# A planned one-core graph kernel: the power iteration recorded ahead of the eigenvector solver, and a narrower window of groups while layer 0 ends

## The chip, the cores and the metric

The kernel runs on one core of a Trainium2 chip. A core has five engines with instruction streams of their own: TensorE (PE in the profile, with PEld for its weight loads), VectorE (DVE), ScalarE (ACT), GpSimd (POOL) and SyncE (SP), which here only issues DMAs. The metric is device time in microseconds, the median of several executions; one more execution is profiled, and every row quoted below comes from that one.

## The reference

The input x holds 128 graphs of 64 nodes with 256 features, in float32; all graphs share one 64x64 adjacency matrix. Four residual layers follow one another, each of them `x = x + f(relu(layernorm(x)))`:

- layer 0: two graph convolutions (`relu(adj @ (h W + b))`), and then, for p = 1, 2, 3, 4, an LSTM over windows of p successive nodes, whose last hidden state replaces the window's last node. The LSTM with p = 4 has four dependent steps;
- layer 1: a spectral graph convolution and an attention block. It needs the largest eigenvalue of the symmetrised adjacency: `L_norm = 2 L / lam_max - I`;
- layer 2: graph attention with an additive score;
- layer 3: a transform into the eigenvector basis of a normalised Laplacian (`U.T @ x`), two dense layers, and the transform back. It needs all 64 eigenvectors.

In short, what bears on this case:

```
x = x + layer0(h, adj, ...)                      # LSTMs, no eigenvalues
lam_max = eigvalsh(L)[-1] + 1e-8                 # layer 1
_, U = eigh(d^-1/2 (diag(deg) - A) d^-1/2)       # layer 3
```

## The kernel before

Nothing is issued as it is written. The code runs once against proxies that record every operation of every engine with its operands (`Plan.record`, line 114), and `Plan.issue` (line 338) then issues all of them in an order that `Plan.schedule` (line 227) works out with a list scheduler. All instructions therefore carry line 344 in the profile, and are told apart by their tiles.

Each recorded operation has a group. Layer 0 is done for eight groups of 1,024 rows (8 tiles of 128 rows), numbered 0 to 7 (`NG = 8`). Group 8 (`WEIGHTS`, line 1390) loads the weights of layers 1 to 3 over those of the LSTMs, and group 9 (`ATTN`) clears four attention tiles. Layers 1 to 3 are done for sixteen groups of 512 rows (4 tiles), numbered 10 to 25 (`REST = 10`, line 1612). The result of layer 0 goes through DRAM: a group of layer 0 writes `put[g]`, and two later groups read it back. The work on the adjacency matrix, the eigenvectors (`eig_decomp`, line 347) and the largest eigenvalue (a power iteration of 21 squarings, lines 1135 to 1156), is one long chain of small operations, mostly on VectorE, and forms group 1000 (`EIG`).

What sets the order:

- the scheduler repeatedly picks, over all engines, the operation that can start first. Among operations that could start at once it takes the lowest rank (`Plan.rank`, line 328): lower groups first, while group `EIG` comes first on TensorE and last on all other engines, and within `EIG` the operation that was recorded earlier comes first;
- an operation is considered only if its group is inside the window above the oldest unfinished group (line 256): `op.group >= oldest + window(oldest) + (op.eng == "SP")` is passed over. DMAs on SP may be one group ahead, and `EIG` is exempt;
- buffers come from pools: 12 tiles `big` of 512 KB, 10 `mid`, 14 `stat` and 8 PSUM banks. While a layer-0 group is the oldest, `reserve` (line 971) holds up to 7 `big` tiles back for it. Ten more `big` tiles are cut from `arena` once `EIG` is finished, and some from `Whh3`, `sums` and `mids` once layer 0 is.

The window before the change reads

```
return max(oldest, 0) + 2 - oldest if oldest < NG - 1 else max(oldest, REST) + 8 - oldest
```

so two groups of layer 0 overlap, and from the moment when group 7 is the oldest, groups up to 17 are inside: eight groups of layers 1 to 3.

Within layer 0, `lstm_step` (line 1213) and `lstm_fast` (line 1261) alternate matmuls into PSUM banks, gate functions on ScalarE and products on VectorE. A group of layers 1 to 3 begins with `fetch` (a DMA), `ln_stats` (line 1195: four `bn_stats` and four `bn_aggr` on VectorE, then four small operations on GpSimd), four ReLUs on ScalarE (`relu_norm`, line 1471) and `mix_fm`, a burst of 32 small matmuls against `lapb`, the scaled Laplacian that the largest eigenvalue gives. The projections with `Wc`, the attention and the rest follow in `layer1` (line 1485). Layer 3 uses `Ub` and `UTb`, the eigenvectors; group 8 also needs them (`ursum`, `C3`, lines 1417 to 1423).

Of the kernel before, what the change touches and what calls it, by code (L numbers as in the profile page):

```python
# [12 lines left out]
N = 64  # L13
# [874 lines left out]
P = 128  # L888
# [3 lines left out]
NG = NT // GT  # L892
HT = 4

SETUP, WEIGHTS, ATTN, REST, EIG = -1, NG, NG + 1, NG + 2, 1000
# [37 lines left out]
def gnn_kernel(ctx: ExitStack, tc: tile.TileContext, a, out):  # L933
# [4 lines left out]
    def C(shape, name):  # L938
        return pool.tile(list(shape), F32, name=name)
# [26 lines left out]
    more(mids, tuple(range(NG)))  # L966

    def window(oldest):
        return max(oldest, 0) + 2 - oldest if oldest < NG - 1 else max(oldest, REST) + 8 - oldest

    def reserve(kind, oldest):
        if oldest < NG:
# [3 lines left out]
    def slack(op):  # L976
        if op.eng == "PE":
            return 0.4 if op.group >= REST and op.group != EIG else 0.12
        return 0.05

    plan = Plan(tc, {"PE": nc.tensor, "V": nc.vector, "ACT": nc.scalar, "G": nc.gpsimd, "SP": nc.sync}, pools, late, reserve, window, EIG, REST + NT // HT - 6, slack)
    PE, V, ACT, G, SP = (plan.proxy(e) for e in ("PE", "V", "ACT", "G", "SP"))

    def bank(name):
        return plan.value("bank")
# [23 lines left out]
    adj2 = C([P, N], "adj2")  # L1009
    adjT2 = C([P, N], "adjT2")  # L1010
# [24 lines left out]
    ident = C([P, P], "ident")  # L1035
    G.iota(ident, pattern=[[1, P]], base=0, channel_multiplier=-1, allow_small_or_imprecise_dtypes=True)
    V.tensor_scalar(ident, ident, 0.0, None, op0=ALU.is_equal)
    ones = C([P, P], "ones")
# [8 lines left out]
    def blockdiag(t):  # L1047
        V.memset(t, 0.0)
        return t[:N, :N], t[N:, N:]
# [54 lines left out]
    Ublk, UTblk = blockdiag(Ub), blockdiag(UTb)  # L1104
    room = Carver(arena)

    QT, Vc, inner = eig_decomp(plan, room, adj2[:N], adjT2[:N], ident[:N, :N], ident, ones)
    for dst, lhs, rhs in ((Ublk, QT, Vc), (UTblk, Vc, QT)):
        l2 = inner.tile([P, 2, N])
        V.tensor_copy(l2, lhs.unsqueeze(1).to_broadcast([P, 2, N]))  # L1110
        pp = bank("U")
        PE.matmul(pp[:, :N], l2.rearrange("p r n -> p (r n)"), rhs, start=True, stop=True)
        V.tensor_copy(dst[0], pp[:N, :N])
        V.tensor_copy(dst[1], pp[N:, :N])


    def colsum(col):

        pt = bank("colsum")
        PE.matmul(pt[:, :1], ones, col, start=True, stop=True)  # L1120
        r = room.tile([P, 1])
        V.tensor_copy(r, pt[:, :1])
        return r
# [30 lines left out]
    V.reciprocal(lmax, lmax)  # L1154
    V.tensor_scalar(lmax, lmax, 2.0, None, op0=ALU.mult)
    V.scalar_tensor_tensor(lapb, adjTb, lmax, ident, op0=ALU.mult, op1=ALU.subtract)


    flat = lambda t: t.rearrange("p t f -> p (t f)")
# [231 lines left out]
    room = Carver(wih[1], whh[1], wih[2], whh[2], wih[0])  # L1391
# [282 lines left out]
```

## Time and profile before

| | |
|---|---|
| median of 3 runs | 2164.6 us (2164.06 to 2165.33) |
| the profiled execution | 2165.9 us, span 2164.1 us |
| TensorE busy | 2112.6 us, 98% of the span |
| VectorE / ScalarE / GpSimd busy | 1800.3 / 1079.8 / 653.1 us |
| matmuls | 16,580 |
| granted TensorE clock, mean | 0.996 |

The span runs from the first to the last instruction on the core. The busy times of an engine are the union of its instructions; two matmuls in the pipeline count once. The table of slices shows one long stretch of layer 0 up to about 1367 us and of layers 1 to 3 after that, with TensorE at nine tenths or more in all slices but the first and the last. A built program's order of instructions can be matched one for one with the trace, engine by engine, and so tells which group an instruction of line 344 belongs to.

### The profile page before, as it was taken

How to read it: one execution, taken by the hardware profiler on the slowest of the kernel's cores; microseconds unless marked ns; L12 is line 12 of the kernel's file. 1: busy time of each engine (PE TensorE's matmuls, PEld its weight loads, DVE VectorE, ACT ScalarE, POOL GpSimd, SP SyncE). 2: the span in 40 equal slices, each digit the busy share in tenths (PEclk: the TensorE clock that was granted, in tenths of full speed). 3: DMA queues.
4: the chain of work that ended last, by engine and by line, in shares of the span. 5: the costliest groups of instructions: out<-in, count | busy, mean ns of one | idle time of the engine just before them, and what ended most of it. 6: DMA issues, size and time to landing. Idle time of an engine off the chain costs nothing.

```text
span 2164.1 us, 45598 instructions
## 1 busy us (share of the span) xinstructions
PE 2112.6 (98%) x16580; PEld 1630.7 (75%) x16580; DVE 1800.3 (83%) x7402; ACT 1079.8 (50%) x2331; POOL 653.1 (30%) x968
## 2 busy tenths in 40 slices
PE   8999999999999999999999999999999999999997
PEld 6688688688678678678778688766777767776776
DVE  5888788889899999899989887568878868885797
ACT  3354354354354354345345345456566655645673
POOL 7221211210200110110110113654456745554353
PEclk9999999999999999999999999999999999999999
DMA  5000100100100100100000213000010000000001
GB/s 205 2 3 22 41 3 22 40 1 21 40 1 20 40 1 20 40 1 21 26 1 23 69 40 97 21 1 2 21 41 21 21 22 21 12 11 11 1 2 60
DMA packets 44866, 57.67 MB, mean 27 GB/s; under 512 B 8928, under 2 KB 38496, under 8 KB 44640
## 3 DMA queue, kind: packets, MB, share of 16 engines
q1 hardware_dynamic: 43536, 53.71, 7.6%
q8 instruction: 130, 2.13, 0.4%
q10 hardware_dynamic: 1104, 1.05, 0.2%
q14 instruction: 96, 0.79, 0.1%
HBM read 37.53 MB, written 16.78 MB: 25 GB/s over the span
## 4 chain that ended last, share of the span: by engine, by line
PE 83%; DVE 11%; POOL 2%; ACT 1%; DMA 1%; issue 1%; SPq 0%; DVEq 0%; ACTq 0%
PE bank L344 83%; DVE arena L344 3%; DVE big L344 3%; DVE stat L344 2%; DVE mids L344 1%; DVE sums L344 1%; POOL stat L344 1%; POOL sums L344 1%; DMA Wih<-in_WihT_dram 1%; ACT mids L344 0%; ACT arena L344 0%; DMA Whh<-in_L_b_dram 0%; DMA big<-put 0%; ACT big L344 0%; SPq L344 0%
## 5 line engine op out<-in xcount | busy, mean ns | idle before, releaser
L344 PE MATMUL bank<-big,Wih 128*128 128x256 f32 (+3 forms) x2400 | 748.2, 435 | 18.7 <-DVE arena L344 9.3
L344 PEld LDWEIGHTS bank<-big,Wih 128*128 128x128 f32 x2400 | 439.9, 190 | 205.0 <-issue 114.4
L344 ACT ACTIVATE mids<-bank,bl 128x256 f32<-128x256 f32 (+3 forms) x528 | 275.4, 528 | 407.3 <-PE bank L344 403.5
L344 PE MATMUL bank<-big,Whh 128*128 128x256 f32 (+2 forms) x1624 | 431.0, 368 | 3.5 <-DVE big L344 3.5
L344 DVE TENSOR_TENSOR arena<-arena 64x21 f32<-64x21 f32 (+5 forms) x2255 | 372.9, 196 | 35.8 <-POOL arena L344 8.2
L344 PEld LDWEIGHTS bank<-big,Whh 128*128 128x128 f32 x1624 | 294.3, 190 | 42.5 <-issue 10.1
L344 PE MATMUL bank<-big,sums 128*128 128x168 f32 (+2 forms) x1728 | 268.8, 307 | 0.0
L344 PEld LDWEIGHTS bank<-big,sums 128*128 128x128 f32 (+1 forms) x1728 | 225.4, 178 | 16.0 <-issue 3.9
L344 POOL TENSOR_SCALAR stat<-stat 128x4 f32<-128x4 f32 (+1 forms) x228 | 67.9, 299 | 485.4 <-DVE stat L344 472.5
L344 ACT COPY mids<-bank 128x168 f32<-128x168 f32 (+2 forms) x393 | 132.1, 357 | 138.1 <-PE bank L344 135.1
L344 DVE TENSOR_TENSOR big<-mids 128x512 f32<-128x512 f32 (+2 forms) x256 | 142.8, 565 | 31.3 <-ACT mids L344 28.6
L344 ACT ACTIVATE mids<-mids,bl 128x336 f32<-128x336 f32 (+2 forms) x192 | 102.4, 540 | 71.4 <-DVE mids L344 67.6
L344 DVE TENSOR_TENSOR mids<-bank,mids 128x168 f32<-128x168 f32 (+2 forms) x307 | 112.9, 372 | 25.8 <-PE bank L344 22.3
L344 DVE SCALAR_TENSOR_TENSOR arena<-arena 64x1 f32<-64x1 f32 (+15 forms) x565 | 120.9, 237 | 7.5 <-POOL arena L344 3.9
L344 POOL TENSOR_TENSOR big<-big 128x168 f32<-128x168 f32 (+1 forms) x24 | 16.8, 712 | 359.9 <-DVE arena L344 132.2
L344 POOL TENSOR_TENSOR stat<-stat,mhalf 128x4 f32<-128x4 f32 (+1 forms) x114 | 122.1, 1072 | 5.7
L344 ACT ACTIVATE mids<-big 128x256 f32<-128x256 f32 (+2 forms) x176 | 89.4, 509 | 67.7 <-DVE big L344 48.8
L344 PE MATMUL bank<-Wih,big 128*128 128x256 f32 (+1 forms) x512 | 111.7, 358 | 0.2 <-ACT big L344 0.2
L344 DVE TENSOR_SCALAR arena<-arena 64x1 f32<-64x1 f32 (+9 forms) x537 | 104.8, 202 | 8.4 <-POOL arena L344 0.8
L344 DVE TENSOR_TENSOR big<-big,mids 128x256 f32<-128x256 f32 (+2 forms) x200 | 99.3, 498 | 11.1 <-ACT mids L344 10.2
L344 PEld LDWEIGHTS bank<-Wih,big 128*128 128x128 f32 x512 | 87.7, 190 | 15.4 <-issue 4.5
L344 ACT COPY big<-bank 128x512 f32<-128x512 f32 x108 | 59.9, 587 | 55.9 <-PE bank L344 50.8
(357 smaller groups left out, 3568.0 us busy)
## 6 DMA issues: line engine op xcount, KB each, us to landing
big<-in_x_dram SPq DMA_DIRECT2D x30, 512.0 KB, 5.2
put<-big SPq DMA_DIRECT2D x16, 512.0 KB, 3.0
Wih<-in_WihT_dram SPq DMA_DIRECT2D x3, 1024.0 KB, 11.8
Whh<-in_WhhT_dram SPq DMA_DIRECT2D x3, 1024.0 KB, 13.8
big<-put SPq DMA_DIRECT2D x6, 512.0 KB, 5.8
arena<-put SPq DMA_DIRECT2D x6, 512.0 KB, 6.6
out_dram<-big SPq DMA_DIRECT2D x12, 256.0 KB, 2.3
out_dram<-arena SPq DMA_DIRECT2D x12, 256.0 KB, 2.3
```

Source lines behind the costliest of these rows:

```text
L344: getattr(self.engines[op.eng], name)(*map(real, args), **{k: real(a) for k, a in kw.items()})
```

## The change

Two edits. The call of `eig_decomp` and the lines that make `Ub` and `UTb` from its result move behind the power iteration, so that the power iteration's operations are recorded first and take their space in `arena` first. No operation is added or removed. And the window has three cases now: with one of groups 7, 8 and 9 the oldest, only group 10 is inside (group 11 for its DMA); from group 10 on, eight groups are, as before.

```diff
     def window(oldest):
-        return max(oldest, 0) + 2 - oldest if oldest < NG - 1 else max(oldest, REST) + 8 - oldest
+        return max(oldest, 0) + 2 - oldest if oldest < NG - 1 else REST + 1 - oldest if oldest < REST else 8
...
     room = Carver(arena)
-
-    QT, Vc, inner = eig_decomp(plan, room, adj2[:N], adjT2[:N], ident[:N, :N], ident, ones)
-    for dst, lhs, rhs in ((Ublk, QT, Vc), (UTblk, Vc, QT)):
-        l2 = inner.tile([P, 2, N])
-        V.tensor_copy(l2, lhs.unsqueeze(1).to_broadcast([P, 2, N]))
-        pp = bank("U")
-        PE.matmul(pp[:, :N], l2.rearrange("p r n -> p (r n)"), rhs, start=True, stop=True)
-        V.tensor_copy(dst[0], pp[:N, :N])
-        V.tensor_copy(dst[1], pp[N:, :N])
-
 
     def colsum(col):
...
     V.scalar_tensor_tensor(lapb, adjTb, lmax, ident, op0=ALU.mult, op1=ALU.subtract)
+
+
+    QT, Vc, inner = eig_decomp(plan, room, adj2[:N], adjT2[:N], ident[:N, :N], ident, ones)
+    for dst, lhs, rhs in ((Ublk, QT, Vc), (UTblk, Vc, QT)):
+        l2 = inner.tile([P, 2, N])
+        V.tensor_copy(l2, lhs.unsqueeze(1).to_broadcast([P, 2, N]))
+        pp = bank("U")
+        PE.matmul(pp[:, :N], l2.rearrange("p r n -> p (r n)"), rhs, start=True, stop=True)
+        V.tensor_copy(dst[0], pp[:N, :N])
+        V.tensor_copy(dst[1], pp[N:, :N])
```

## The prediction

> **What bounds the kernel now.** I read the page first, then busy time by stretch, then TensorE's waits where layer 0 ends, then the timelines of TensorE and VectorE at those waits.
>
> The page, engines:
>
> ```profile
> PE 2112.6 (98%) x16580; PEld 1630.7 (75%) x16580; DVE 1800.3 (83%) x7402; ACT 1079.8 (50%) x2331; POOL 653.1 (30%) x968
> ```
>
> TensorE is the bound, with 51.5 us of idle time in all; an edit that leaves its matmuls alone can win no more than part of that. Where it lies (stretch, length, then busy time and count of PE, PEld, DVE, ACT, POOL, the granted clock and the DMAs):
>
> ```profile
> 50.00:1200.00 1150.00, 1138.77 (x6765) 895.97 (x6764) 1023.94 (x5008) 520.75 (x1309) 161.80 (x289) 1.00 0.06 18
> 1200.00:1250.00 50.00, 46.36 (x182) 34.01 (x182) 43.26 (x200) 17.30 (x36) 10.79 (x20) 0.97 0.22 74
> 1250.00:1300.00 50.00, 45.96 (x259) 40.09 (x258) 44.99 (x187) 23.73 (x60) 5.72 (x9) 1.00 0.15 44
> 1300.00:1350.00 50.00, 49.00 (x257) 43.40 (x256) 37.82 (x180) 26.06 (x61) 15.03 (x16) 1.00 0.32 104
> 1350.00:1400.00 50.00, 46.63 (x633) 39.88 (x632) 27.12 (x72) 25.41 (x52) 32.00 (x44) 1.00 0.06 23
> 1400.00:1950.00 550.00, 541.19 (x5910) 395.82 (x5912) 440.76 (x1173) 326.00 (x567) 302.02 (x398) 1.00 0.06 17
> ```
>
> Between 1200 and 1400 us TensorE is idle for 12.0 us; this is where group 7 runs alone and layer 0 ends. The waits there, and TensorE's timeline around them:
>
> ```profile
> PE bank L344 <- DVE big L344: 5.3, 5, 2.5
> PE bank L344 <- issue: 3.4, 2, 1.7
> PE bank L344 <- DVE mids L344: 1.7, 2, 1.2
> PE bank L344 <- DVE arena L344: 1.6, 2, 1.2
> ...
> 1223.19 10.97 PE L344 MATMUL bank<-big,Wih 128*128 128x512 f32 x26 [1.16 <-DVE arena L344]
> 1237.51 0.78 PE L344 MATMUL bank<-big,Whh 128*128 128x256 f32 x2 [2.48 <-DVE big L344]
> 1264.10 7.33 PE L344 MATMUL bank<-big,Wih 128*128 128x336 f32 x26 [1.60 <-DVE big L344]
> 1363.00 1.16 PE L344 MATMUL bank<-lapb,big 64*64 64x64 f32 x64
> 1371.06 1.44 PE L344 MATMUL bank<-lapb,arena 64*64 64x64 f32 x83 [1.72 <-issue]
> ```
>
> Eight groups of layers 1 to 3 are allowed in from 1222 us, but their first matmul is the burst at 1363.00. In the trace, group 10 has its row statistics at 1230, while its ReLUs run at 1309.55: the eight inputs and the tiles reserved for group 7 leave no `big` tile for its result. So the wide window brings TensorE nothing before 1363. It brings VectorE work, though:
>
> ```profile
> 1228.41 0.43 DVE L344 BATCH_NORM_STATS2 stat<-big 128x6 f32<-128x256 f32 x1 [1.30 <-DMA big<-put]
> 1233.12 1.37 DVE L344 BATCH_NORM_STATS2 stat<-big 128x6 f32<-128x256 f32 x4
> 1236.80 0.66 DVE L344 TENSOR_TENSOR big<-mids 128x512 f32<-128x512 f32 x1
> ```
>
> The statistics of groups 10 to 13 stand between group 7's products (the row at 1236.80 is one), and the matmul at 1237.51 waits for that product. The chain's two values, last:
>
> ```profile
> L344 DVE SCALAR_TENSOR_TENSOR lapb<-adjTb,arena,ident x1: 333/333/333, 131.1 to 131.1; 128x128 f32<-128x128 f32 x1
> L344 DVE COPY Ub<-bank x2: 208/218/228, 1337.0 to 1337.2; 64x64 f32<-64x64 f32 x2
> ```
>
> `lapb` is there at 131 us, 1230 us before its first use; the eigenvectors at 1337, some 29 us before group 7 ends at 1366.6.
>
> [...]for 1.30 us VectorE sits before a `bn_stats` whose DMA is under way, with group 7's products behind it. [...]Here 2.48 us sufficed: the next ten 256-column matmuls start 0.43 us apart and not 0.216, so the gap costs 1.9 us more. [...]
>
> **The power iteration ahead.** No instruction is added or removed, and `lapb` isn't waited for: worth nothing by itself. But the eigenvector chain falls behind. By the order of instructions, ahead of group 6's last VectorE instruction stand 3,897 of group `EIG` before and 3,832 after. 65 x 0.19 us (small `arena` operations, start to start) = 12.4 us of VectorE work moves under group 7. The cover is the 29 us above; in the new order the chain's last matmul still has 11 us of matmuls after it before group 7 ends.
>
> **The narrow window, while layer 0 ends.** Three things move ahead of group 7's end, all of group 10: its burst (1.44 us by its usual pace), sixteen matmuls of 256 columns for `Wc` (x 0.216 = 3.46) and eight transposes (x 0.11 = 0.88), together 5.8 us of TensorE work. They stand about where TensorE waited 2.48, 1.60 and 0.69 us. The statistics of groups 11 to 13 (3 x 1.6 us of VectorE, start to start) leave the 1230s. Four group-7 matmuls of 0.86 us (3.4 us) slip from before group 6's last transpose to after it, which alone shifts work and wins nothing.
>
> The interval from group 6's last transpose (1220.2) to group 7's (1365.2) took 145.0 us for 131.2 us of matmuls at their usual spacing, so 13.8 us were idle or at the slow clock. After: 131.2 + 3.4 + 5.8, less the burst of group 10 that already stood there (1.4), = 139.0. Its first part, up to the first matmul of the eigensolver's last phase (before at 1292.65), decides. It held 60.8 us of matmuls in 72.5; VectorE had 65.9 us of work after group 6's four additions, and 4.8 us besides. After, it holds 74.0 us of matmuls and, counting instructions in the new order at their measured spacing, 74.5 us of VectorE. Adding the additions (1.8) and, say, 4 us of VectorE's own waits gives 80.3 us, 6.3 above the matmuls. The other two parts had 2.1 us of such time; I leave 2.6. Sum: 8.9 against 13.8, a gain of 4.9 us.
>
> **What comes after layer 0.** Before, seven bursts and more follow each other and TensorE waits 3.4 us on "issue"; in the new order no more than two do, so those waits go. But groups 11 to 17 now start cold. Group 11 (its input is loaded) needs 1.6 us of statistics, 0.30 + 1.08 + 0.27 + 0.30 and handovers (2.2) on GpSimd, four ReLUs 0.49 us apart with three copies between (3.2): its burst can start 8 us after group 7's last matmul. Over that time group 10 has eight 512-column products (6.9 us), five 256-column ones (2.2) and its score burst (1.4): 10.5 us. Groups 12 and 13 load behind two stores; the first such load took 5.6 us, and 1.6 + 2.2 + 3 us later, 13.4 in all, their bursts are ready, while TensorE arrives after 16.7. So the start is covered on paper; I charge 3.0 us for small gaps (bounds: 0, all covered; 11, nothing covered from the load to the burst). Gain 0.4 us. From 1960 us on, TensorE's order is the same in both: nothing.
>
> Total: 4.9 + 0.4 = 5.3 us. The span of 2164.1 lies 0.5 below the median, so the median becomes 2164.6 - 5.3 = about 2159.
>
> **Rivals.** *VectorE eats the gain* (about 2164, chance 0.12): the 12.4 us arriving under group 7 delay its products, and TensorE keeps its 13.8 us. For: VectorE is 45.0 us busy of 50 at 1250 to 1300. Against: this work is last in rank and goes where VectorE has room.
>
> *The cold start isn't covered* (slower, 2169 to 2176, chance 0.12): [...]group 10's softmax stands behind the statistics of groups 12 and 13, which wait for loads issued only after layer 0. If these land some 4 us late, group 10 stops too, and TensorE sees the whole path of load, statistics, GpSimd, ReLUs: 5.6 + 1.6 + 2.2 + 3 = 12 us, less the 5.3. It decides once the idle time after group 7 passes 3.0 + 5.3 = 8.3 us.
>
> *The eigenvectors come late* (about 2172, chance 0.06): group 8 needs them, and the window opens only after it. They must lose the whole 29 us, where I count 12.
>
> *More is gained* (2146 to 2154, chance 0.20): group 10 also closes the remaining waits and shortens the slow clock: up to 13.8 + 3.4 = 17 us.
>
> **How the numbers follow.** The likeliest case has 0.50, with its own range 2154 to 2162. A measurement of this kernel can tell about 0.2%, 4.3 us, from no change, so "faster" is below 2160.3: four fifths of this case and all of the largest gain, 0.40 + 0.20 = 0.60. "Same": 0.10 + 0.12 = 0.22. "Slower": 0.12 + 0.06 = 0.18. The range 2148 to 2171 leaves out the ends of the outer cases.
>
> **What would show it.** Matmuls on `lapb` at about 1235, filling or shortening the 2.48 us gap, the clock whole after it; matmuls on `Wc` before 1275; `Ub` at 1345 to 1355; group 7's last store about 1 us earlier than now or level; no two "issue" waits of 1.7 us; less than 4 us idle in the 30 us after layer 0. A gap there from "DMA big<-put" or from VectorE's `stat` behind it would make me wrong, as would `Ub` after 1362.

## The result, and the profile after

The changed kernel takes 2162.5 us (median of 14 executions, 2159.2 to 2164.9); the kernel before, run beside it, 2165.3 us. The ratio is 0.9984, with a 95% interval of 0.9976 to 0.9992: a gain of 2.9 us, about half of what was forecast, and below the 0.2% that was called the limit of what can be told. The profiled execution took 2164.9 us, 2.4 us over the median. Its span is 2163.1 us, 1.0 less than before, so the comparison of the two traces has to explain 1.0 us; the other 1.9 are spread between executions and are not placed. One thing about them is on record: the profiled execution has the lowest mean clock of its fourteen, 0.993 (the others 0.994 to 0.997).

TensorE is still busy for 98% of the span. The stretches around the end of layer 0, as before (length, then PE, PEld, DVE, ACT, POOL with counts, granted clock, DMA share, GB/s):

```profile
1200.00:1250.00 50.00, 48.32 (x249) 34.34 (x248) 41.53 (x211) 21.25 (x42) 5.61 (x8) 1.00 0.17 56
1250.00:1300.00 50.00, 47.60 (x273) 42.52 (x272) 44.82 (x184) 23.58 (x59) 5.21 (x9) 1.00 0.16 51
1300.00:1350.00 50.00, 45.84 (x231) 40.11 (x230) 35.44 (x166) 20.34 (x47) 10.45 (x11) 1.00 0.17 45
1350.00:1400.00 50.00, 47.41 (x572) 38.37 (x572) 34.80 (x119) 25.84 (x51) 29.14 (x46) 0.97 0.27 96
```

Between 1200 and 1300 TensorE is busy for 3.6 us more than before and its clock is whole. From 1300 to 1350 it is busy for 3.2 us less. TensorE's timeline after, at the places in question (start, length, what, and in brackets the idle time ahead of it and who ended it):

```profile
1232.67 1.47 PE L344 MATMUL bank<-lapb,big 64*64 64x64 f32 x64
...
1244.09 0.67 PE L344 MATMUL bank<-big,Wih 128*128 128x256 f32 x2 [1.12 <-DVE arena L344]
...
1318.03 0.70 PE L344 MATMUL bank<-big,Whh 128*128 128x256 f32 x2 [2.61 <-DVE big L344]
...
1382.57 5.21 PE L344 MATMUL bank<-Wih,big 128*128 128x256 f32 x16 [2.57 <-ACT big L344]
```

Group 10's burst stands at 1232.67, where TensorE had waited 2.48 us. Two new gaps stand against that. At the first, VectorE's timeline reads

```profile
1312.51 0.43 DVE L344 TENSOR_TENSOR big<-mids 128x256 f32<-128x256 f32 x1 [1.10 <-ACT mids L344]
1316.93 0.23 DVE L344 TENSOR_SCALAR Whh<-Whh 128x128 f32<-128x128 f32 x1 [3.99 <-DMA Whh<-in_L_b_dram]
```

The second row is the negation of layer 3's bias, `nb3a` (group 8, line 1416). It waits 3.99 us for its load, and group 7's products wait behind it. In the kernel before, the same instruction reads

```profile
1316.45 0.23 DVE L344 TENSOR_SCALAR Whh<-Whh 128x128 f32<-128x128 f32 x1 [1.85 <-DMA Whh<-in_L_b_dram]
```

VectorE stood there for 1.85 us, and it cost TensorE 0.47. The load lands at about the same time in both (1316.4 and 1316.9); VectorE now comes 1.6 us earlier.

At the second gap, VectorE's and then ScalarE's timeline:

```profile
1375.27 1.41 DVE L344 BATCH_NORM_STATS2 stat<-big 128x6 f32<-128x256 f32 x4 [1.93 <-DMA big<-put]
```

```profile
1379.02 1.09 ACT L344 ACTIVATE arena<-big,stat 128x256 f32<-128x256 f32 x2 [3.36 <-POOL stat L344]
1380.01 0.56 ACT L344 COPY big<-bank 128x512 f32<-128x512 f32 x1
1380.48 0.60 ACT L344 ACTIVATE arena<-big,stat 128x256 f32<-128x256 f32 x1
1380.98 1.54 ACT L344 COPY big<-bank 128x512 f32<-128x512 f32 x3
```

Group 12's input is loaded only after group 7's stores, and lands at 1375.3. Its statistics, GpSimd's four operations and its ReLUs follow one another, and the ReLUs (1379.02) stand in ScalarE's queue ahead of the copies of group 11's burst (1380.01 and the last of the three from 1380.98), whose matmuls had ended at 1378.5. TensorE waits for the second copy.

The eigenvectors, from the tile's instructions:

```profile
L344 DVE COPY Ub<-bank x2: 217/222/228, 1355.8 to 1356.1; 64x64 f32<-64x64 f32 x2
```

One measure makes all kernels comparable: for each matmul, the time to the next one's start, less the usual spacing for its columns (0.0225 us for 64 columns in the bursts, 0.11 for 128, 0.142 for 168, 0.216 for 256, 0.283 for 336, 0.429 for 512). Summed, the usual spacing is 2106.5 us in every kernel here; what is over is idle time and slow clock. It can come out below zero where the pace is better than usual. By the slow clock is meant here a run of matmuls that start about twice the usual spacing apart with no idle time between them (0.43 us for 256 columns, after the gap that ends at 1237.51 in the kernel before); it falls differently from one trace to the next, and moves a column by 1.7 us in the row of before and by 2.9 in that of the changed kernel (both below). The ends of the span add 5.6 us. The table holds it by stretch, worked out from one trace each, with the medians and ratios of all runs (a median is to be compared through its ratio, as the kernel before came to 2165.3 to 2166.2 us beside the different groups of runs):

| kernel | median us | ratio to before, 95% | to 1200 | 1200-1350 | 1350-1450 | 1450-2100 | rest | sum |
|---|---|---|---|---|---|---|---|---|
| before | 2165.3 | | 29.2 | 17.4 | 2.1 | -6.0 | 9.2 | 52.0 |
| changed | 2162.5 | 0.9984 (0.9976-0.9992) | 28.9 | 13.5 | 7.5 | -9.0 | 10.2 | 51.0 |
| e1: window alone | 2163.3 | 0.9990 (0.9984-0.9997) | 28.2 | 15.9 | 6.1 | -8.7 | 10.9 | 52.3 |
| e2: recording order alone | 2176.1 | 1.0041 (1.0029-1.0053) | 29.8 | 15.1 | -0.5 | 7.8 | 10.6 | 62.8 |
| e3: changed, nb3a on GpSimd | 2160.5 | 0.9974 (0.9963-0.9984) | 27.4 | 11.7 | 5.2 | -7.4 | 9.1 | 45.9 |
| e5: changed, two groups | 2180.3 | 1.0065 (1.0053-1.0077) | 31.5 | 21.9 | 10.1 | -3.4 | 10.6 | 70.6 |
| e6: before, nb3a on GpSimd | 2163.9 | 0.9993 (0.9987-0.9999) | 27.8 | 15.4 | 2.2 | -5.6 | 9.2 | 48.9 |
| e7: e3, group 12 loaded ahead | 2162.9 | 0.9991 (0.9982-0.9999) | 30.8 | 16.2 | 3.4 | -1.9 | 9.4 | 57.8 |
| e8: e3, groups 12, 13 loaded ahead | 2168.0 | 1.0003 (0.9995-1.0011) | 29.3 | 14.1 | 0.2 | 2.4 | 8.6 | 54.6 |
| e9: e3, two groups, fewer tiles held | 2169.6 | 1.0016 (1.0010-1.0023) | 26.2 | 19.3 | 2.0 | -0.6 | 8.5 | 55.4 |
| e10: e3, ReLUs behind copies | 2161.2 | 0.9973 (0.9964-0.9983) | 28.6 | 10.5 | 6.4 | -7.5 | 8.8 | 46.8 |
| e11: e3, planning number 0.44 | 2163.8 | 0.9987 (0.9979-0.9995) | 28.7 | 11.7 | 5.4 | -4.0 | 9.3 | 51.1 |
| e12: e1, nb3a on GpSimd | 2165.0 | 0.9993 (0.9986-0.9999) | 29.5 | 15.4 | 4.5 | -9.1 | 9.3 | 49.6 |
| e13: e3, seven groups | 2175.1 | 1.0040 (1.0027-1.0052) | 29.4 | 11.7 | 3.0 | 8.8 | 8.3 | 61.1 |

Of the changed kernel, against before: 3.9 us gained from 1200 to 1350, 5.4 lost from there to 1450, 3.0 gained from there to 2100, and 0.6 lost in the other two columns together: 1.0 us in all, but for rounding. Two of these hold slow clock. Of the 17.4 us in the row of before, 1.7 are slow clock, and e6 has the same order and an equal gap without it (below). Of the 7.5 us from 1350 to 1450 in the row of the changed kernel, 2.9 are slow clock: 1.2 after the gap that ends at 1382.57, and 1.7 after short waits from 1409 to 1412, which e3 has without it.

### The profile page after: what moved, and what is told of

The parts are those of the page before. It is cut to its first block, busy times and chain, and to the rows that moved or that the text cites. A ratio compares the mean times of both kernels' runs of the same rounds, so it can differ in the third digit from the quotient of the medians.

```text
span 2163.1 us, 45587 instructions
## 1 busy us (share of the span) xinstructions
PE 2117.6 (98%) x16580; PEld 1632.8 (75%) x16580; DVE 1795.0 (83%) x7402; ACT 1066.5 (49%) x2321; POOL 650.6 (30%) x968
## 5 line engine op out<-in xcount | busy, mean ns | idle before, releaser
L344 DVE TENSOR_TENSOR arena<-arena 64x21 f32<-64x21 f32 (+5 forms) x2251 | 372.1, 195 | 29.8 <-POOL arena L344 1.3
L344 ACT COPY mids<-bank 128x168 f32<-128x168 f32 (+2 forms) x378 | 124.8, 349 | 147.7 <-PE bank L344 142.9
L344 ACT ACTIVATE mids<-mids,bl 128x336 f32<-128x336 f32 (+3 forms) x192 | 102.0, 539 | 77.6 <-DVE mids L344 73.6
L344 DVE TENSOR_TENSOR mids<-bank,mids 128x168 f32<-128x168 f32 (+1 forms) x294 | 103.1, 356 | 8.4 <-PE bank L344 4.7
L344 DVE TENSOR_SCALAR arena<-arena 64x1 f32<-64x1 f32 (+8 forms) x533 | 103.1, 200 | 8.4 <-POOL arena L344 0.4
L344 DVE TENSOR_TENSOR big<-big,mids 128x256 f32<-128x256 f32 (+2 forms) x192 | 93.7, 488 | 11.0 <-ACT mids L344 10.0
L344 POOL TENSOR_TENSOR arena<-arena 64x1 f32<-64x1 f32 x66 | 44.8, 678 | 152.6 <-ACT arena L344 106.3
L344 DVE BATCH_NORM_STATS2 stat<-big 128x6 f32<-128x256 f32 x228 | 83.2, 406 | 4.9 <-DMA big<-put 4.0
L344 ACT COPY big<-bank 128x512 f32<-128x512 f32 x90 | 49.5, 586 | 58.0 <-PE bank L344 55.9
## 6 DMA issues: line engine op xcount, KB each, us to landing
Whh<-in_WhhT_dram SPq DMA_DIRECT2D x3, 1024.0 KB, 13.8
```

The source lines that it names most:

```text
L344: getattr(self.engines[op.eng], name)(*map(real, args), **{k: real(a) for k, a in kw.items()})
```

## The experiments

### Which edit does it: e1 and e2

The kernel before with the window alone (e1), and with the recording order alone (e2):

```
e1:  -  ... else max(oldest, REST) + 8 - oldest
     +  ... else REST + 1 - oldest if oldest < REST else 8
e2:  QT, Vc, inner = eig_decomp(...) and the lines of Ub, UTb moved behind the power iteration
```

> The kernel before with the window edit alone; the eigenvectors stay recorded ahead of the power iteration. Theory A (the window carries all of the effect, the recording order is worth nothing): 2162.5 us, within 1.5 of the changed kernel; no gap of 2.5 us at 1235, TensorE idle for some 2.6 us at 1380 as in the changed kernel. Theory B (the recording order carries it, by moving 12 us of VectorE work): 2165, as before. Theory C (the recording order costs, because 65 VectorE instructions of the eigenvector chain are pushed under group 7 and its products come later): 2159 to 2160.5, with the last phase of the eigensolver ending some 10 us earlier than in the changed kernel (about 1345 instead of 1355.6).

> The recording order alone; the window of eight groups stays. Theory A: 2165 us, within 1.5 of the kernel before; the statistics of several groups stay between group 7's products near 1235 and TensorE waits 2 us or more there. Theory B: 2162.5. Theory C: 2166.5 to 2168, since VectorE has 12 us more work under group 7.

Measured: e1 2163.3 us, near theory A; e2 2176.1, 9 us slower than before and outside all three theories. The gap near 1235, TensorE's timeline of e1 and then of e2:

```profile
1235.60 0.70 PE L344 MATMUL bank<-big,Whh 128*128 128x256 f32 x2 [1.52 <-DVE big L344]
```

```profile
1236.07 0.70 PE L344 MATMUL bank<-big,Whh 128*128 128x256 f32 x2 [1.13 <-DVE big L344]
```

It was 2.48 us before. Neither edit alone fills it. With the window alone group 10's burst comes at 1259.0; only with both is it at 1232.7, since group 10's statistics then start on VectorE at 1225.75 instead of 1227.29 and group 7's matmuls are placed differently around them. In the column 1200 to 1350 the window comes out at 1.5 us, the order at 2.3, both together at 3.9. But the row of before holds 1.7 us of slow clock there. TensorE just after its gap in the kernel before, then the gap and the same four matmuls in e6, whose order of TensorE is that of before up to 1316:

```profile
1238.08 1.91 PE L344 MATMUL bank<-big,sums 128*128 128x256 f32 x4
```

```profile
1236.04 0.70 PE L344 MATMUL bank<-big,Whh 128*128 128x256 f32 x2 [2.46 <-DVE big L344]
1236.57 1.03 PE L344 MATMUL bank<-big,sums 128*128 128x256 f32 x4
```

Eight matmuls lost 0.21 us each after the gap in one trace, and none after an equal gap in the other. With these 1.7 us taken out, the window alone gains nothing in this stretch (15.9 us against 15.7), the order alone 0.6, and both together 2.2. With the window in place, the order adds 2.4 us (15.9 in e1, 13.5 in the changed kernel). So the two edits win here only together.

And yet e2 is slow: the 13.8 us that it loses lie between 1450 and 2100. From 1450 to 1800 its TensorE waits 7.1 us for VectorE in nine waits for `big` and `arena`, where the changed kernel waits 2.3 us in six. No eigenvector work is left by then. What differs is the order of the groups of layers 1 to 3, which the scheduler has chosen anew. In the changed kernel, e1, e3 and e12 this order is the same instruction for instruction on all engines, and their column reads -9.0, -8.7, -7.4 and -9.1: a given order repeats within 1.7 us. Before and e6 share another order, at -6.0 and -5.6.

### The wait before nb3a: e3, e6 and e12

```
-    V.tensor_scalar(nb3a, nb3a, -1.0, None, op0=ALU.mult)
+    G.tensor_scalar(nb3a, nb3a, -1.0, None, op0=ALU.mult)
```

on the changed kernel (e3), on the one before (e6), and on the window alone (e12).

> The changed kernel with one operation on another engine: the negation of layer 3's bias (nb3a) goes from VectorE to GpSimd, so VectorE doesn't stand 4.0 us before it at 1313 to 1317 for its load. Theory A (that wait is the cause of TensorE's gap of 2.6 us at 1315.4): the gap falls below 0.6 us and the time to 2160, 2 to 3 us below the changed kernel. Rival (group 7's products are late for other reasons, VectorE being 45 us busy of 50; or GpSimd stands there instead and holds group 10's additions): the gap moves to another product and the time stays at 2162.5 within 1.

> The kernel before with nb3a's negation on GpSimd. There VectorE stood 1.9 us before it, but TensorE only 0.47 us. Theory A (that wait became dear only because the change leaves VectorE and group 7 closer together): within 0.5 us of the kernel before, 2165. Rival (taking this operation off VectorE is worth 2 us wherever it stands): 2163.

> The kernel before with the window edit and nb3a on GpSimd, the eigenvectors recorded first as before. Theory A (the recording order is worth nothing by itself): 2160.5, within 1 us of the same with the eigenvectors recorded second. Rival B (recording the eigenvectors second is worth 1 us or more, since VectorE then has less to do ahead of group 6's end and TensorE's matmuls there come earlier): 2161.5 to 2163. Rival C (it costs, the eigenvectors ending 10 us later): 2158 to 2159.5.

Measured in e3: 2160.5 us, as theory A has it. The intervals of the two ratios, 0.9963 to 0.9984 and 0.9976 to 0.9992, just overlap, so the cause rests on the trace. GpSimd's timeline:

```profile
1315.36 0.55 POOL L344 TENSOR_SCALAR Whh<-Whh 128x128 f32<-128x128 f32 x1 [2.73 <-DMA Whh<-in_L_b_dram]
```

GpSimd now stands 2.73 us before the same load and nothing of group 7 is behind it; from 1300 to 1350 TensorE is busy for 2.5 us more than in the changed kernel (48.34 against 45.84), and it has no gap at that matmul: the order of its instructions is the same in both kernels, and 2.77 us are gone at that one place. In e6 the ratio is 0.9993, and its interval, 0.2 to 2.8 us below before, holds both theories. The traces decide for theory A: TensorE's column is 2.0 us lower than before, of which 0.47 is this wait and the rest the slow clock at 1238, which has nothing to do with `nb3a`. In e12 the wait is gone as well, 1.25 us in e1, but the ratios (0.9993, and e1's 0.9990) can't tell 1.25 us from nothing, and 1.5 us of slow clock just ahead of it in e12's trace hide it in the column. So by the traces the wait's price follows how closely TensorE and VectorE run: 0.47 us before, 1.25 with the window, 2.77 with both edits (beyond the usual spacing). The length of VectorE's own wait doesn't set it alone, as that was 1.85 us in e1 as it was before.

e12 against e3 is also the recording order's second test: 0.9993 against 0.9974, with intervals that don't meet. That is rival B in kind, some 4 us, though e12's 2165.0 lies beyond the range that B gave. The traces differ by 3.7 us between 1200 and 1350, of which 1.5 are slow clock in e12. Theory A, that the order is worth nothing, has fallen for the narrow window; for the wide one the 0.6 us of e2 don't show it.

### The start of the groups after layer 0: e5, e7, e8, e9, e10

e5 lets two groups in while layer 0 ends:

```
-  REST + 1 - oldest if oldest < REST else 8
+  REST + 2 - oldest if oldest < REST else 8
```

> The changed kernel with two groups inside the window instead of one while layer 0 ends (12 for its load): group 11's statistics are done ahead of layer 0's end, but group 10's sixteen Wc matmuls are no longer placed there. Theory A (after layer 0 the groups start cold): TensorE's gap of 2.6 us at 1380 and the slow clock behind it go, 3 to 4 us; 3.5 us less of group 10's work fills the gaps under group 7, which gives back up to 3: 2160.5 to 2162.5. Rival (the gap at 1380 is not group 11's late start): it stays, and the time is 2163 to 2165.

It took 2180.3 us, 18 more than the changed kernel. Neither theory allowed for that. Group 7 loses 8.4 us between 1200 and 1350 against the changed kernel, 4.4 of them at the slow clock, with four operations of group 10 on TensorE in place of seventeen; then the groups start in a bunch, and ScalarE's timeline shows

```profile
1393.02 2.07 ACT L344 ACTIVATE arena<-arena,stat 128x256 f32<-128x256 f32 x4 [6.10 <-POOL stat L344]
```

with TensorE idle for 4.9 us behind it. e9 asks whether the seven `big` tiles held back for group 7 are the reason. It has five (and nb3a on GpSimd):

```
-  return {"big": 7, "mid": 5, ...
+  return {"big": 7 if oldest < NG - 1 else 5, "mid": 5, ...
```

> Two groups inside the window while layer 0 ends, as in the run that was 15 us slower than before, but with five big tiles held back for group 7 instead of seven, and nb3a on GpSimd. Group 10's sixteen Wc matmuls are then ahead of group 7's end again, and nine operations of group 11 besides. Theory A (that run was slow because the tiles held back starved both groups, so that groups 11 to 16 then started in step and TensorE waited for one bunch of statistics): 2157 to 2162. Rival (two groups' statistics between group 7's products cost TensorE 5 us or more by themselves): 2170 or more.

Measured: 2169.6 us. The bunch is gone (2.0 us in 1350 to 1450), so that half was the tiles. The column 1200 to 1350 isn't mended: 19.3 us, 7.6 over e3 (2.6 of them at the slow clock), with seventeen operations of group 10 there again and nine of group 11 besides. Letting a second group in between group 7's products costs TensorE more than it fills. That fits the rival, whose bound of 2170 is missed by less than half a microsecond. Whether group 11's statistics on VectorE do it, as the rival has it, or its operations on the other engines was not separated.

e7 and e8 leave the window at one group and let only inputs in, group 12's or 12's and 13's, with five tiles held back as in e9:

```
-  ... >= oldest + self.window(oldest) + (op.eng == "SP"):
+  ... >= oldest + self.window(oldest) + (op.eng == "SP") * (2 if 7 <= oldest < 10 else 1):     # e8: 3
```

> The previous experiment's kernel with the negation on GpSimd, and group 12's input (DMA alone) let in while layer 0 ends, with five instead of seven big tiles held back for group 7 so that it has a place. Theory A (ScalarE stands 3.4 us before group 12's ReLUs, whose input lands late, with group 11's copies behind them): ScalarE's wait at 1379 and TensorE's gap of 2.5 us at 1380 go; 1350 to 1450 falls by 2 to 3 us, and the time to 2157 to 2159 if the order after 1450 is no worse. Rival (group 11's own path of statistics, GpSimd and ReLUs sets the gap): the gap stays above 2 us and the time at 2160.5.

> As the run with group 12's input, but group 13's input is let in as well. Theory A: the first gap goes as there; the second (0.65 and 0.66 us at 1409 to 1412, with the slow clock behind) depends on groups 14 to 16 and may stay: 2157 to 2159, within 1 us of that run. Rival (each further load ahead fills more): 1 us or more below it.

The start gets better as theory A says: TensorE's time beyond the usual pace from 1350 to 1450 falls from 5.2 us (e3) to 3.4 and 0.2. The total gets worse, 2162.9 and 2168.0 us against 2160.5, and again the loss is after 1450: -1.9 and 2.4 instead of -7.4. (e7's profiled execution was 8.9 us over its median, so its columns are too high.) The order after layer 0 is a new one in both.

e10 avoids that. It takes e3's order as planned, and moves four instructions by hand:

```
+  late = [o for o in order if o.index in (10619, 10620, 10621, 10789)]   # three ReLUs of group 12, one addition
+  order = [o for o in order if o not in late]
+  i = next(i for i, o in enumerate(order) if o.index == 10622)           # the fourth ReLU
+  order[i:i] = late
```

> The changed kernel with nb3a on GpSimd and four instructions moved by hand, everything else in the same order: three of group 12's ReLUs on ScalarE, and the GpSimd addition that reads behind them, go behind group 11's two copies, so the copies no longer stand behind ReLUs whose input lands late. Theory A (ScalarE's in-order queue makes TensorE's gap of 2.5 us at 1376 to 1379): the gap falls below 1 us, the slow clock behind it goes, and the time to 2157 to 2158.5, 2 to 3.5 us below the kernel with nb3a on GpSimd (2160.5). Rival (the next engine in the chain fills the time): the gap moves a few us later and the time stays at 2160 to 2161.

TensorE's timeline at the gap, in e3 and in e10 (where the added lines shift the line number):

```profile
1378.68 5.41 PE L344 MATMUL bank<-Wih,big 128*128 128x256 f32 x16 [2.54 <-ACT big L344]
```

```profile
1377.42 2.86 PE L348 MATMUL bank<-Wih,big 128*128 128x256 f32 x12 [1.22 <-ACT big L348]
```

The gap is halved, and the clock from 1350 to 1400 is whole (1.00, in e3 0.97); the two together bring TensorE 3.0 us. What is left of the gap is the time of three copies after the burst, the last of which ends at 1377.4. So ScalarE's queue is shown as the cause of half the gap, a little less than theory A had it. The total doesn't move: ratio 0.9973 against 0.9974. The order of TensorE's instructions is the same in both, so they can be laid side by side, and 2.3 of the 3.0 us are lost again between the end of these sixteen matmuls and 1400. More than half of that is in one burst, in e3 and then in e10:

```profile
1385.00 1.11 PE L344 MATMUL bank<-lapb,big 64*64 64x64 f32 x64
```

```profile
1382.32 2.29 PE L348 MATMUL bank<-lapb,big 64*64 64x64 f32 x64
```

In e10 the burst pauses every 0.49 us, the spacing of ScalarE's six ReLUs at that time (from 1381.69 on), and the matmuls after its transposes wait 0.38 us for ScalarE. That is the rival's mechanism: the gap moves a few microseconds on. A further 1.8 us from 1400 to 1420 go with a lower granted clock (0.97 from 1400 to 1450, in e3 1.00), as described at the end.

### Is it the order after 1450: e11 and e13

e11 changes a number that only the scheduler's planning uses, e13 the number of groups inside the window once group 10 is the oldest; both on e3.

```
e11:  -  return 0.4 if op.group >= REST and op.group != EIG else 0.12
      +  return 0.44 if op.group >= REST and op.group != EIG else 0.12
e13:  -  ... if oldest < REST else 8
      +  ... if oldest < REST else 7
```

> The changed kernel with nb3a on GpSimd, and the allowance for handovers that the scheduler uses for TensorE in layers 1 to 3 0.44 instead of 0.40; it is a number in the planning only. The order is the same up to group 7's end and differs in some 1,200 of TensorE's 4,390 operations after it. Theory A (the time after 1450 us hangs on the order that the list scheduler happens to find, by several us in either direction): TensorE's time beyond its matmuls' usual pace between 1450 and 2100 changes by 3 us or more against -7.4 us, and the time leaves 2159.5 to 2161.5. Rival (such orders are worth the same, and the earlier runs' losses there come from what their edits mean): 2160.5 within 1.

> The changed kernel with nb3a on GpSimd and seven instead of eight groups inside the window once group 10 is the oldest. The order is the same up to group 7's end and some 75 TensorE operations beyond. Theory A (the order found after 1450 is worth several us either way): the time leaves 2159.5 to 2161.5, the part before 1400 within 1 us of the same kernel with eight. Rival: 2160.5 within 1.

Measured: 2163.8 and 2175.1 us, 3 and 15 over e3, with 11.7 us in all three from 1200 to 1350, and -4.0 and 8.8 against -7.4 after 1450. The stretch from 1450 to 1600 in e13, then in e3:

```profile
1450.00:1600.00 150.00, 136.41 (x1406) 100.15 (x1406) 116.23 (x334) 78.66 (x139) 68.67 (x98) 0.99 0.05 16
```

```profile
1450.00:1600.00 150.00, 148.66 (x1683) 111.17 (x1682) 118.54 (x335) 83.37 (x151) 73.38 (x101) 1.00 0.05 16
```

In e13 TensorE is idle for 13.6 us, in five gaps of 1.0 to 3.2 us between 1571 and 1593 above all. e11's change has no meaning for the hardware; it only makes the planner choose anew. Theory A holds: what the list scheduler finds for layers 1 to 3 comes out from -9.1 to 8.8 us over these kernels, more than anything that the change does in its own place. e11 alone is a neutral test, worth 3.4 us in that column. In e13 one group less leaves TensorE less work to choose from, and how much of its 16.2 us is that was not separated. Why one order is better than another was not settled beyond the gaps named.

## Why the prediction was right or wrong

- **The first part of group 7's interval**, from group 6's last transpose to the eigensolver's last phase: forecast 80.3 us for 74.0 us of matmuls; the trace has 79.8. Right.
- **The other parts** were given 2.6 us beyond the matmuls. The whole interval took 150.9 us for the forecast 139.0 of work, 11.9 over against 8.9 forecast (before, between the same marks, 145.4 for 131.2, 14.2 over). This failed by 3 us, by one wait that I didn't name: `nb3a`'s load. In e3, without it, the interval takes 148.5, 9.5 over, and the gain of 4.9 us that was forecast comes out as 4.7. Of the 14.2 us before, though, 1.7 are the slow clock after the gap at 1237.5. The prediction read it as ten matmuls 0.43 us apart and 1.9 us, and as a cost of the gap; there are eight, and e6 has the gap without the cost. Part of what was to be won was one execution's. The step that failed is "I leave 2.6": it took the later parts' small waits for granted, and the 1.85 us that VectorE stood there before were in none of the rows that I read.
- **The power iteration ahead, "worth nothing by itself"**: wrong where the window is narrow. There the order lets group 10's statistics start on VectorE earlier (1225.75 instead of 1227.29), and the traces show some 2.3 us for it between 1200 and 1350 (2.4 in the changed kernel against e1, 2.2 in e3 against e12 without e12's slow clock). I counted the 12.4 us that arrive late and not the time that they leave free. What I put down to the window needs both edits: the window alone gains nothing in that stretch.
- **The eigenvectors** come at 1355.8, 18.8 us later than before, where 12.4 was counted and 1345 to 1355 forecast. The cover held: nothing waits for them.
- **What comes after layer 0**: forecast a gain of 0.4 us (3.4 gained at the two "issue" waits, 3.0 charged). The two waits (1.72 and 1.65 us) are gone, as said; the trace doesn't name what made them. The stretch from 1350 to 1450 loses 5.4 us all the same, so the start costs 5.4 + 3.4 = 8.8 and not 3.0. The covering work was counted in sum, 10.5 us, and its order on ScalarE wasn't: the late load of group 12 holds the copies of group 11. That is the named sign against the forecast, VectorE's `stat` behind "DMA big<-put", though it reaches TensorE through GpSimd and ScalarE. The rival *the cold start isn't covered* had this mechanism and a threshold of 8.3 us; 7.5 came, 2.9 of them at the slow clock, of which the forecast had none. (The sum for groups 12 and 13 also has a slip: 5.6 + 1.6 + 2.2 + 3 is 12.4, not 13.4. It changes nothing.)
- **"From 1960 us on, nothing"**: right within a microsecond (0.4 us between 1950 and the end). But between 1450 and 1950 I costed nothing either, and there the new order wins 2.5 us. It was luck of the order, as e2 and e11 show with the other sign. This term, of plus or minus several microseconds, was missing from the sum and from the range's reasons.
- **The signs**: `lapb` matmuls at 1232.7 and a whole clock after them, `Wc` matmuls at 1258.8, no "issue" wait of 1.7 us, and 2.6 us of idle time in one wait in the 30 us after layer 0, all as named. Group 7's last VectorE operation ends 1.8 us later than before (1369.0) and not earlier, as `nb3a`'s wait lies ahead of it.
- **The total**: forecast 5.3 us of gain, measured 2.9 by the medians, inside the range and on the side of "no change that can be told". A wait not named, a start mis-sized by 5.8 and an order not foreseen, the last one in the change's favour, make the difference. That a gain is left at all owes much to that last one: in these two traces the start takes back more (5.4 us) than group 7's stretch gives (3.9).

The fastest version measured is e3, level with e10: the changed kernel with one operation moved to GpSimd, 2160.5 us, ratio 0.9974. It is clear of the kernel before; from the changed kernel its interval is not quite separate.

## What to carry to other kernels

When an edit takes slack out of a stretch, read the waits there that cost little before: a wait of 1.85 us on a load cost TensorE 0.47; once the engines ran closer, it was 3.99 us and cost 2.77, and putting that one instruction on an engine with nothing urgent behind it took the cost away. Where a list scheduler orders the work, a local edit can reorder everything behind it, so measure a neutral perturbation of the planner first: here it moved the time by 3 us, as much as the whole change. Before a difference between two traces is credited to an edit, look for matmuls at the slow clock in each of them: here they made up 1.7 of the 3.9 us. And test a cause with the planned order held and a few instructions moved by hand, or the reordering will answer instead of the cause.

## What the runs showed of the hardware

**A small GpSimd operation took 4.24 us while VectorE ran six operations.** In e7 TensorE had a gap of 3.61 us at 1703.9, behind ScalarE, which had waited 4.26 us for GpSimd. GpSimd's timeline, then VectorE's over the same time:

```profile
1695.52 4.24 POOL L344 TENSOR_SCALAR stat<-stat 128x4 f32<-128x4 f32 x1
```

```profile
1695.46 1.20 DVE L344 TENSOR_TENSOR sums<-sums,Wih 128x1024 f32<-128x1024 f32 x1
1696.57 0.69 DVE L344 SCALAR_TENSOR_TENSOR big<-big,mids 128x512 f32<-128x512 f32 x1
1697.17 1.29 DVE L344 SCALAR_TENSOR_TENSOR big<-big,sums 128x512 f32<-128x512 f32 x2
1698.38 1.29 DVE L344 TENSOR_TENSOR big<-big,Wih 128x512 f32<-128x512 f32 x2
1699.58 1.29 DVE L344 TENSOR_TENSOR sums<-bank,Wih 128x512 f32<-128x512 f32 x2
```

An operation on four columns that takes 0.23 us elsewhere (for one, at 1703.54) took 4.24. It began as VectorE began six operations with two inputs in SBUF (0.06 us after the first), and ended (1699.76) when VectorE turned to one that reads PSUM (`bank`, at 1699.58). The changed kernel has a shorter case, GpSimd's row and then VectorE's:

```profile
1854.37 2.24 POOL L344 TENSOR_SCALAR stat<-stat 128x4 f32<-128x4 f32 x1
```

```profile
1854.30 0.41 DVE L344 TENSOR_TENSOR mids<-mids,stat 128x256 f32<-128x256 f32 x1
1854.63 0.68 DVE L344 SCALAR_TENSOR_TENSOR arena<-arena,mids 128x512 f32<-128x512 f32 x1
1855.23 1.28 DVE L344 TENSOR_TENSOR big<-big,stat 128x512 f32<-128x512 f32 x2
1856.43 0.37 DVE L344 BATCH_NORM_AGGREGATE stat<-stat 128x2 f32<-128x6 f32 x4
```

Here the 2.24 us span four operations with two inputs in SBUF, and end (1856.61) as VectorE turns to one with a single input. That VectorE holds GpSimd up there is read from these times alone; no run changed one of the two by itself.

**The same gaps had the slow clock behind them in one trace and not in another.** It followed a gap of 2.48 us in the kernel before (granted clock 0.97 from 1200 to 1250), and not one of 2.46 us at the same place in e6: the same four matmuls took 1.91 and 1.03 us (rows under e1 and e2). Shorter gaps show it too. The changed kernel and e3 have the same instructions and waits here (0.65 us, three of 0.16 to 0.17, then 0.66 or 0.67). TensorE after, then e3:

```profile
1412.44 1.64 PE L344 MATMUL bank<-Wih,mids 128*128 128x256 f32 x4 [0.66 <-ACT mids L344]
1413.88 7.40 PE L344 MATMUL bank<-mids,Whh 128*128 128x512 f32 x14
```

```profile
1408.76 1.13 PE L344 MATMUL bank<-Wih,mids 128*128 128x256 f32 x4 [0.67 <-ACT mids L344]
1409.72 6.17 PE L344 MATMUL bank<-mids,Whh 128*128 128x512 f32 x14
```

The eighteen matmuls take 1.7 us longer after. The granted clock from 1400 to 1450 is 0.97 in the changed kernel, e1 and e10, and 1.00 in e3 and e12. So these two places moved a trace by 1.7 us each with no edit to account for it, and a difference of that size between two traces shows nothing by itself.
